# Query splits on GpSimd, value copies on ScalarE, and the first maxima reduced over two banks, in a graph layer followed by 128-head attention

## The chip, the cores and the metric

The kernel runs on one core of a Trainium2 chip. The metric is the device time of one execution in microseconds (us). Its engines have short names in the profile: PE is TensorE (matmuls), PEld its weight loads, DVE is VectorE, ACT is ScalarE, POOL is GpSimd, and SP is SyncE, which here only issues transfers (DMAs). Each engine works through its own queue in order, and waits on semaphores of the others. SBUF is the on-chip memory of 128 partitions; PSUM is the matmuls' output memory, in banks of 512 float32 for each partition.

## The reference

There are 3327 nodes with 128 features and a sparse weighted adjacency matrix `adj` (about 5 entries in a row). Layer 0 is a graph layer, layer 1 an attention of 128 heads of 8 numbers each:

```python
def reference(x, adj, W_in, W_out, Wq, Wk, Wv, Wo):
    x = _layernorm(x + _L0_gnn_ref(x, adj, W_in, W_out))
    x = _layernorm(x + _L1_gnn_ref(x, adj, adj, Wq, Wk, Wv, Wo))

def _L0_gnn_ref(X, A, W_in, W_out):
    return _message(X, A, W_in) + _message(X, A.T, W_out)   # A rows divided by their sum, then @ X @ W

def _L1_gnn_ref(x, spatial_encoding, edge_encoding, Wq, Wk, Wv, Wo):
    n, d = x.shape                         # 3327, 128
    h = Wq.shape[0] // d                   # 8
    q = (x @ Wq.T).reshape(d, n, h)
    k = (x @ Wk.T).reshape(d, n, h)
    v = (x @ Wv.T).reshape(d, n, h)
    a = jnp.einsum('dnh,dmh->dnm', q, k) * d ** (-0.5)
    a = jax.nn.softmax(a + spatial_encoding + edge_encoding, axis=2)
    out = jnp.einsum('dnm,dmh->dnh', a, v).reshape(n, h * d)
    return out @ Wo.T
```

The reshape to `(d, n, h)` cuts the flat product, so the rows of one tile of nodes belong to several heads: two tiles of 128 rows hold nearly ten heads.

## The kernel before

**Stages.** First layer 0 (lines 173 to 332): the matrix streams in twice, and PE sums it against x. Then the projections (lines 642 to 735) compute queries, keys and values of all nodes and store them in device memory. Then comes attention (lines 740 to 1325): a short opening in which the maxima of the first group of four heads are found alone, and a long loop of scores, exponentials and products (lines 1255 to 1325), in which the maxima of later groups are found beside. At the end the results are joined, projected and normalized.

**Projections.** Nodes are taken in 13 pairs of tiles (`t`), each with two halves (`s`), so 26 tiles of 128 rows. For a tile PE makes three products of 128x1024 into PSUM (line 689: `wq`, `wk`, `wv`). ACT copies queries and keys out (`full`, line 697). Both are then split into three bfloat16 parts whose sum is the float32 value (lines 712 to 717): the first part is a rounded copy on ACT (line 714), `left` is what remains (line 715, DVE), the second part is its rounded copy (line 716, ACT), the third what remains of that (line 717, DVE). The tile `left` has three buffers, `parts` three (one for queries, one for keys of a pair), `full` four. At the second half SP stores the parts (line 719, to `q_d` and `k_d`). A float32 copy goes out too: of queries by a copy on POOL (line 700), of keys by one on ACT (line 702), both stored by DMAs that POOL issues (line 703). Of the keys ACT takes squares (line 708), DVE sums them to sizes (line 710), and POOL issues their store (line 711). Values are copied out of PSUM by DVE (line 692) into one of two buffers `v_sb`, and SP stores them (line 693).

**Beside the projections** two threshold searches run (`early_of`, `select`, lines 440 to 574), one for 4 heads, one for 28. They look for the largest keys of each head: DVE compares all sizes with a middle value and counts (lines 472, 476), PE sums the counts over partitions (line 481), DVE moves the bounds (lines 493 to 503), ten times for each of two limits. Then keys get ranks (PE lines 535 and 536, DVE line 537), and the chosen keys of the first two groups are gathered by products with one-hot rows (`hots_of` line 608 on DVE, `fill_tile` line 617 on PE) after POOL has split them (`split_keys`, lines 595 to 598). In this stage a scheduler sets the order on each engine, by its own estimate of times; the program's order is only its start.

**First maxima.** For each group an item of work is one tile of queries and 512 chosen keys for two heads (`run_item`, lines 999 to 1035): two matmuls into two single banks of the pool `ps_m` (three banks), and two reductions by DVE, one for each bank. Until the first group's maxima are stored, items run one after another (line 1202) with nothing beside them but small steps (`fix`, `merge`). The pool `ps_e` (two buffers of two banks) is taken by scores (line 1271) once the long loop begins. From here on the order on each engine is written out by hand.

Of the kernel before, what the change touches and what calls it, by code (L numbers as in the profile page):

```python
# [9 lines left out]
F32 = mybir.dt.float32  # L10
# [4 lines left out]
ALU = mybir.AluOpType  # L15
AX = mybir.AxisListType
# [4 lines left out]
P = 128  # L21
# [4 lines left out]
H = 8  # L26
HEADS = D
G = NP * D
NB = 512
# [49 lines left out]
def gnn_layers(ctx: ExitStack, tc: tile.TileContext, x, adj, adjt, w_in, w_out, wq, wk, wv, wo, out):  # L79


    nc = tc.nc
# [85 lines left out]
    with ExitStack() as c0:  # L168
# [4 lines left out]
        with ExitStack() as c1:  # L173
# [102 lines left out]
            for t0 in range(0, NT, 2):  # L276
# [7 lines left out]
                    op=ALU.is_equal,  # L284
# [110 lines left out]
        groups, queries, for_maxima, stored = {}, {}, {}, set()  # L395
# [182 lines left out]
        def load_choice(pool, s):  # L578

            assert ranked.get(s) == NT  # L580
            first = max(f for f in rank_d if f <= s * GH)
            at = pool.tile([P, NT, GH], F32, name="at", bufs=2)
            nc.sync.dma_start(at, rank_d[first][:, s - first // GH])
            keys = pool.tile([P, GH, NT, H], F32, name="keys")
            for j in range(GH):
                head = (s * GH + j) * N
                nc.sync.dma_start(keys[:, j], kf_d[head : head + NP, :].rearrange("(p t) h -> p t h", t=NT))
            return at, keys
# [49 lines left out]
        def begin_fill(banks):  # L638
            for which in range(2):
                nc.tensor.matmul(banks[which], ident_b, nothing, start=True, stop=False)  # L640

        with ExitStack() as c1:
            stage = c1.enter_context(tc.tile_pool(name="stage", bufs=2, side="right"))
            vbuf = c1.enter_context(tc.tile_pool(name="vbuf", bufs=1, side="right"))
            ps_pr = c1.enter_context(tc.tile_pool(name="ps_pr", bufs=4, space=PSUM))
            v_sb = [vbuf.tile([P, D, VW], F32, name=f"v_sb{i}") for i in range(2)]
            for v in v_sb:
                nc.gpsimd.memset(v, 1.0)

            chooser = c1.enter_context(tc.tile_pool(name="chooser", bufs=1, side="right"))  # L650

            def early_of(first, n, g):
                yield from select(chooser, lambda: ps_pr.tile([P, H * D], F32, name="pr"), first, n, first)
                at, keys = load_choice(chooser, g)
                parts = split_keys(chooser, keys)
                yield
                packed = chooser.tile([P, KEPT], BF16, name="packed")
                for u in range(TCUTS):
                    pair = ps_pr.tile([P, H * D], F32, name="pr")
                    banks = [pair[:, :NB], pair[:, NB:]]  # L660
                    begin_fill(banks)
                    tiles = tiles_of_fill(u)
                    for t in tiles:
                        fill_tile(banks, parts, hots_of(chooser, at, t, 8), u, t, t == tiles[-1])
                        yield
                    end_fill(banks, packed, u)
                spread(g, packed)
                begin_all(("s", g))

            info = chooser.tile([P, NT, 2 * SLOTS], F32, name="info")  # L670
            for t in range(NT):
                nc.gpsimd.indirect_dma_start(
                    info[:, t], None, info_d, bass.IndirectOffsetOnAxis(ap=node[:, t : t + 1], axis=0)
                )
            nc.gpsimd.tensor_copy(near, info[:, :, :SLOTS])
            nc.gpsimd.tensor_copy(weight, info[:, :, SLOTS:])

            choosing = [(early_of(*EARLY[0], 0), 1, 8), (early_of(*EARLY[1], 1), 4, 9)]
            for t in range(NT // 2):
                g = slice(2 * t * P * D, 2 * (t + 1) * P * D)  # L680
                parts_of = {}
                for name in ("wq", "wk"):
                    parts_of[name] = stage.tile([P, PARTS, H, 2, D], BF16, name="parts", bufs=3)
                for s in range(2):
                    for name in ("wq", "wk", "wv"):
                        pr = ps_pr.tile([P, H * D], F32, name="pr")
                        rows = x1t[:, 2 * t * P : 2 * (t + 1) * P].rearrange("d (p s) -> d s p", s=2)[:, s]
                        for c, w in bank_cuts(H * D):
                            nc.tensor.matmul(pr[:, c : c + w], rows, ws[name][:, c : c + w], start=True, stop=True)
                        if name == "wv":  # L690
                            v = v_sb[s]
                            nc.vector.tensor_copy(v[:, :, :H], pr.rearrange("p (c h) -> p c h", h=H))
                            nc.sync.dma_start(v_d[g, :].rearrange("(p s c) w -> p s c w", p=P, s=2)[:, s], v)
                            continue

                        full = stage.tile([P, H, D], F32, name="full", bufs=4)
                        nc.scalar.mul(full.rearrange("p h c -> p (h c)"), pr, 0.5 * D**-0.5 if name == "wq" else 1.0)
                        flat = stage.tile([P, D, H], F32, name="flat", bufs=3)
                        if name == "wq":
                            nc.gpsimd.tensor_copy(flat, full.rearrange("p h c -> p c h"))  # L700
                        else:
                            nc.scalar.copy(flat, pr.rearrange("p (h c) -> p c h", h=H))
                        nc.gpsimd.dma_start(
                            (qf_d if name == "wq" else kf_d)[g, :].rearrange("(p s c) h -> p s c h", p=P, s=2)[:, s], flat
                        )
                        if name == "wk":
                            square = stage.tile([P, H, D], F32, name="square", bufs=1)
                            nc.scalar.activation(square.rearrange("p h c -> p (h c)"), pr, AF.Square)
                            size = stage.tile([P, D], F32, name="size")
                            nc.vector.tensor_reduce(size, square.rearrange("p h c -> p c h"), axis=AX.X, op=ALU.add)  # L710
                            nc.gpsimd.dma_start(size_d[g].rearrange("(p s c) -> p s c", p=P, s=2)[:, s], size)
                        sb = parts_of[name]
                        left = stage.tile([P, H, D], F32, name="left", bufs=3)
                        nc.scalar.copy(sb[:, 0, :, s], full)
                        nc.vector.tensor_sub(left, full, sb[:, 0, :, s])
                        nc.scalar.copy(sb[:, 1, :, s], left)
                        nc.vector.tensor_sub(sb[:, 2, :, s], left, sb[:, 1, :, s])
                        if s:
                            nc.sync.dma_start(
                                (q_d if name == "wq" else k_d)[:, g].rearrange("r (p c) -> p r c", p=P),  # L720
                                sb.rearrange("p a h s c -> p (a h) (s c)"),
                            )

                    for some, begins, times in choosing:
                        if t >= begins:
                            for _ in range(times):
                                next(some, None)
                group_of(0)
                for _ in range(4 if t else 0):
                    begin_next()  # L730
            for some, _, _ in choosing:
                for _ in some:
                    pass
            nc.scalar.activation(gain, weight, AF.Exp, scale=-2.0)
            nc.vector.tensor_scalar(gain, gain, -1.0, 1.0, op0=ALU.mult, op1=ALU.add)
# [4 lines left out]
    with c_att as c1:  # L740
# [5 lines left out]
        ps_e = c1.enter_context(tc.tile_pool(name="ps_e", bufs=2, space=PSUM))  # L746
        ps_m = c1.enter_context(tc.tile_pool(name="ps_m", bufs=3, space=PSUM))
# [223 lines left out]
        def run_item(kind, g, of, *where):  # L971
# [25 lines left out]
                yield  # L997
                return
            spend(dve=1.37)
            banks = [ps_m.tile([P, NB], F32, name="m") for _ in range(2)]  # L1000
            kept = k_kept[g % 2]
            rows = [slice(64 * (1 - y), 64 * (1 - y) + KR) for y in range(2)]
            if kind != "maxima":
                q, c = where
# [16 lines left out]
            mx, i, x, c = where  # L1021
            tile_of = slice(i, NP, NT) if of.shape[-1] == NP else slice(i * P, (i + 1) * P)
            c0 = 0 if c < TCUTS else TCUTS
# [6 lines left out]
                    stop=True,  # L1030
                )
            yield
            for y in range(2):
                nc.vector.tensor_reduce(mx[:, i, y, c - c0 : c - c0 + 1], banks[y], axis=AX.X, op=ALU.max)  # L1034
            yield

        chosen_all = []
# [156 lines left out]
        with tc.manual_schedule(engines={ENG.PE, ENG.Activation, ENG.DVE, ENG.Pool, ENG.SP}):  # L1194
# [60 lines left out]
            for g in range(NG):  # L1255
                for b, (n0, w) in enumerate(BLOCKS):
# [9 lines left out]
                    for t in range(NT):  # L1266
                        pt = P if t < NT - 1 else P - (NP - N)
                        e = [None] * GH
                        for x0 in range(0, 2, per):
# [12 lines left out]
                            m = iter(())  # L1282
# [5 lines left out]
                            if busy:  # L1288
                                taken += 1
                                m = next_item()  # L1290
# [310 lines left out]
```

## Time and profile before

| | us |
|---|---|
| three runs | 12242.42, 12248.63 (median), 12254.28 |
| the profiled execution's own time | 12249.46 |
| its span | 12247.8 |
| PE busy | 11301.5 (92%) |
| ACT busy | 10801.5 (88%) |
| DVE busy | 9320.2 (76%) |
| POOL busy | 3389.2 (28%) |

The profile is of one execution. Its span leaves out what lies before the first and after the last instruction. Busy shares are averages over stages that differ much: in 40 slices of 306 us each, of which a digit is the busy share in tenths, the first four hold layer 0, the projections and the opening of the attention:

```profile
PE   6646999999999999999999999999999999999986
DVE  9678787878787788788888887888788888777306
ACT  6431899999989999999999999999999999999993
POOL 0221111111111124444443344343434334211002
```

From the fifth slice on PE and ACT are over 90% busy; before it no engine is all the time. Line numbers stand as L692 for line 692; an arrow `out<-in` names tiles by the program's names.

### The profile page before, as it was taken

What the parts mean: (1) busy time and instruction counts of PE and PEld (TensorE: products, weight loads), DVE (VectorE), ACT (ScalarE), POOL (GpSimd) and SP (SyncE); (2) the same over time, 40 slices, a digit from 0 to 9 for tenths busy, and PEclk for the clock granted to TensorE, in tenths of its full rate; (3) what the DMA queues carried; (4) which work ended last, traced back from release to release, by engine and by line L of the source; (5) the groups of instructions that cost most, each with busy time, mean ns of one, the idle gap of its engine ahead of it and who ended that gap; (6) DMA issues with size and microseconds to landing.
All of it is one profiled execution on the core that took longest, in us unless ns stands there. A gap on an engine that the chain in (4) does not pass through costs nothing.

```text
span 12247.8 us, 237994 instructions
## 1 busy us (share of the span) xinstructions
PE 11301.5 (92%) x90246; PEld 3038.3 (25%) x90246; DVE 9320.2 (76%) x18121; ACT 10801.5 (88%) x11375; POOL 3389.2 (28%) x4073
## 2 busy tenths in 40 slices
PE   6646999999999999999999999999999999999986
PEld 3321222222222222222222222222222222222214
DVE  9678787878787788788888887888788888777306
ACT  6431899999989999999999999999999999999993
POOL 0221111111111124444443344343434334211002
PEclk8765999999999999999999999999999999999997
DMA  6562444444431122222222222222222222222104
GB/s 229 159 160 67 40 42 40 40 40 35 41 35 22 31 51 71 67 59 62 61 60 62 60 64 66 62 56 71 61 67 56 62 59 61 59 59 56 29 7 131
DMA packets 2221820, 783.21 MB, mean 64 GB/s; under 512 B 1844208, under 2 KB 2111475, under 8 KB 2213941
## 3 DMA queue, kind: packets, MB, share of 16 engines
q1 hardware_dynamic: 2137109, 434.44, 22.7%
q0 software_dynamic: 78816, 286.92, 7.4%
q10 hardware_dynamic: 4736, 46.52, 1.1%
q8 instruction: 712, 11.67, 0.4%
q14 instruction: 447, 3.66, 0.1%
HBM read 597.12 MB, written 187.86 MB: 64 GB/s over the span
## 4 chain that ended last, share of the span: by engine, by line
ACT 37%; PE 33%; issue 12%; DVE 9%; DMA 1%; SPq 0%; POOL 0%; ACTq 0%; DVEq 0%; POOLq 0%
ACT es L1295 35%; PE o L1225 17%; PE e_ps L1275 11%; DVE mx_top L1034 4%; PE m L1025 3%; DVE mx_rest L1034 1%; PE y L1353 1%; ACT es L1297 1%; DVE hot L608 1%; DVE o_sb L1234 0%; PE m L617 0%; PE m L1170 0%; DVE above L472 0%; SPq L418 0%; PE m L640 0%
## 5 line engine op out<-in xcount | busy, mean ns | idle before, releaser
L1295 ACT ACTIVATE es<-e_ps 128x1024 f32<-128x1024 f32 (+1 forms) x9984 | 9469.8, 1023 | 648.0 <-PE e_ps L1275 364.3
L1225 PE MATMUL o<-es,v 128*9 128x512 f32 x46592 | 5760.2, 567 | 33.2 <-DVE o_sb L1234 32.7
L1034 DVE TENSOR_REDUCE mx_top<-m 128x1 f32<-128x512 f32 x6656 | 4252.7, 684 | 1207.1 <-PE m L1025 1162.7
L1275 PE MATMUL e_ps<-q_e,k_st 50*128 50x512 bf16 (+1 forms) x23296 | 4270.8, 370 | 224.6 <-ACT es L1295 81.9
L1275 PEld LDWEIGHTS <-k_st 50*128 50x128 bf16 (+1 forms) x23296 | 1413.9, 95 | 6257.5 <-issue 5787.9
L1034 DVE TENSOR_REDUCE mx_rest<-m 128x1 f32<-128x512 f32 x2048 | 1308.8, 683 | 371.9 <-PE m L1025 367.7
L1025 PE MATMUL m<-k_kept,q_m 48*128 48x512 bf16 x6656 | 1428.0, 385 | 103.7 <-DVE mx_top L1034 53.1
L608 DVE TENSOR_SCALAR hot<-hot_no,at 128x336 bf16<-128x336 bf16 x3840 | 1297.4, 404 | 224.8 <-PE m L617 209.3
L844 POOL TENSOR_TENSOR slot_each<-hits,whole_q 128x832 f32<-128x832 f32 x256 | 425.6, 1662 | 2987.4 <-DVE hits L829 2972.3
L1225 PEld LDWEIGHTS o<-es,v 128*9 128x9 f32 x46592 | 696.2, 88 | 1557.6 <-issue 1443.6
L1297 ACT ACTIVATE es<-e_ps 128x1020 f32<-128x1020 f32 x832 | 809.2, 1024 | 72.9 <-PE e_ps L1275 54.1
L1025 PEld LDWEIGHTS <-q_m 48*128 48x128 bf16 x6656 | 508.7, 144 | 160.0 <-issue 153.7
L1234 DVE COPY o_sb<-o 128x512 f32<-128x512 f32 (+1 forms) x224 | 145.1, 648 | 527.9 <-PE o L1225 525.9
L1075 POOL DMA_INDIRECT near_rows<-kn_d,near x211 | 201.3, 954 | 1062.0 <-DVE prod L1085 985.4
L1025 PE MATMUL m<-k_kept,slot_rows_q 48*128 48x512 bf16 x2048 | 442.5, 385 | 33.1 <-DVE mx_rest L1034 26.4
L798 POOL TENSOR_TENSOR slot_each<-whole_q 128x416 f32<-128x416 f32 x64 | 57.8, 904 | 1462.7 <-DMA whole_q<-qf_d 1418.9
L1147 POOL TENSOR_TENSOR acc<-acc,prod 128x1024 f32<-128x1024 f32 x185 | 430.5, 2327 | 14.5
L242 PE MATMUL acc<-a_t,x 128*128 128x512 f32 (+1 forms) x728 | 311.3, 584 | 64.1 <-DMA a_t<-in_adj_dram 44.0
L1146 POOL TENSOR_TENSOR prod<-near_rows,s 128x1024 f32<-128x1024 f32 x185 | 365.9, 1978 | 2.5
L617 PE MATMUL m<-hot,parts 128*24 128x168 bf16 (+9 forms) x7200 | 289.3, 230 | 38.1 <-DVE hot L608 37.7
L1075 POOL DMA_INDIRECT near_rows<-vn_d,near x211 | 206.9, 981 | 346.5 <-DVE prod L1085 295.7
L1085 DVE TENSOR_TENSOR prod<-qn,near_rows 128x512 f32<-128x512 f32 x422 | 294.9, 699 | 0.0
(301 smaller groups left out, 6127.0 us busy)
## 6 DMA issues: line engine op xcount, KB each, us to landing
q_m<-q_d SPq DMA_DIRECT2D x768, 52.0 KB
q_e<-q_d SPq DMA_DIRECT2D x2304, 16.0 KB
a_t<-in_adj_dram ACTq DMA_DIRECT2D x13, 1663.5 KB
a_t<-in_adj_dram SPq DMA_DIRECT2D x13, 1663.5 KB
a_t<-in_adjt_dram SPq DMA_DIRECT2D x13, 1663.5 KB
a_t<-in_adjt_dram ACTq DMA_DIRECT2D x13, 1663.5 KB
q_d<-parts SPq DMA_DIRECT2D x13, 1536.0 KB
k_d<-parts SPq DMA_DIRECT2D x13, 1536.0 KB
```

Source lines behind the costliest of these rows:

```text
L242: nc.tensor.matmul(acc[:, b, :w], x0[:, t, :], a_t[:, n0 : n0 + w], start=t == 0, stop=t == NT - 1)
L608: nc.vector.tensor_scalar(hot, hot_no, at[:, t, j : j + 1], None, op0=ALU.is_equal)
L844: nc.gpsimd.tensor_mul(each, hits[y][:, i : i + 4, :, None].to_broadcast(shape), whole_q[:, y, None].to_broadcast(shape),)
L1025: nc.tensor.matmul(banks[y], of[rows[y], tile_of], kept[rows[y], x, c * NB : (c + 1) * NB], start=True, stop=True,)
L1034: nc.vector.tensor_reduce(mx[:, i, y, c - c0 : c - c0 + 1], banks[y], axis=AX.X, op=ALU.max)
L1075: nc.gpsimd.indirect_dma_start(rows.rearrange("p d h -> p (d h)"), None, table, bass.IndirectOffsetOnAxis(ap=rows_at, axis=0))
L1146: nc.gpsimd.tensor_mul(prod, vg, share)
L1147: nc.gpsimd.tensor_add(acc[:, :, :H], acc[:, :, :H], prod)
L1225: nc.tensor.matmul(o[32 * j : 32 * j + VW, :w], v4[:pt, j, t, :], e[j][:pt], start=t == 0, stop=t == NT - 1,)
L1275: nc.tensor.matmul(bank[:pt, y, x * NB // per : x * NB // per + w], k[r, x0 + x, t * P : t * P + pt], q[r, x0 + x, :w], start=True, stop=True,
L1295: nc.scalar.activation(es[:pt, :, :w], bank[:pt, :, :w], AF.Exp, scale=2.0)
L1297: nc.scalar.activation(es[:pt].rearrange(shape, x=per)[:, :, :, :w], bank[:pt].rearrange(shape, x=per)[:, :, :, :w], AF.Exp, scale=2.0,)
```

## The change

There are three edits. Value copies out of PSUM go from DVE to ACT. The last three steps of the split of queries, two subtractions and a rounded copy, go to POOL (before: DVE, ACT, DVE); keys are split as before. And until the first group's maxima are stored, an item's two matmuls write two banks of one buffer of `ps_e`, and one reduction takes both banks to two numbers.

```diff
                         if name == "wv":
                             v = v_sb[s]
-                            nc.vector.tensor_copy(v[:, :, :H], pr.rearrange("p (c h) -> p c h", h=H))
+                            nc.scalar.copy(v[:, :, :H], pr.rearrange("p (c h) -> p c h", h=H))
                             nc.sync.dma_start(v_d[g, :].rearrange("(p s c) w -> p s c w", p=P, s=2)[:, s], v)
...
                         nc.scalar.copy(sb[:, 0, :, s], full)
-                        nc.vector.tensor_sub(left, full, sb[:, 0, :, s])
-                        nc.scalar.copy(sb[:, 1, :, s], left)
-                        nc.vector.tensor_sub(sb[:, 2, :, s], left, sb[:, 1, :, s])
+                        if name == "wq":
+                            nc.gpsimd.tensor_sub(left, full, sb[:, 0, :, s])
+                            nc.gpsimd.tensor_copy(sb[:, 1, :, s], left)
+                            nc.gpsimd.tensor_sub(sb[:, 2, :, s], left, sb[:, 1, :, s])
+                        else:
+                            nc.vector.tensor_sub(left, full, sb[:, 0, :, s])
+                            nc.scalar.copy(sb[:, 1, :, s], left)
+                            nc.vector.tensor_sub(sb[:, 2, :, s], left, sb[:, 1, :, s])
...
             spend(dve=1.37)
-            banks = [ps_m.tile([P, NB], F32, name="m") for _ in range(2)]
+            pair = None
+            if (0, 0) not in stored and kind == "maxima":
+                pair = ps_e.tile([P, 2, NB], F32, name="e_ps")
+                banks = [pair[:, y] for y in range(2)]
+            else:
+                banks = [ps_m.tile([P, NB], F32, name="m") for _ in range(2)]
...
-            for y in range(2):
-                nc.vector.tensor_reduce(mx[:, i, y, c - c0 : c - c0 + 1], banks[y], axis=AX.X, op=ALU.max)
+            if pair is not None:
+                nc.vector.tensor_reduce(mx[:, i, :, c - c0], pair, axis=AX.X, op=ALU.max)
+            else:
+                for y in range(2):
+                    nc.vector.tensor_reduce(mx[:, i, y, c - c0 : c - c0 + 1], banks[y], axis=AX.X, op=ALU.max)
```

In the built program the order that the scheduler makes changes too. SP's queue has both stores of a pair's parts behind POOL's or DVE's last split. POOL's split of the gathered keys of the first group (lines 595 to 598) stands behind the splits of tile 8; before, it stood ahead of the copy of tile 7. SP's loads of the sizes for the search of 28 heads stand behind the values of tile 8; before, part of them stood behind the values of tile 6. On DVE the first instruction of a tile is now the sum of squares (line 710); before, it was the first subtraction of the queries.

## The prediction

> **What bounds the kernel now.** I read the busy time by stage first (columns: stretch in us; busy us of PE, its weight loads, DVE, ACT, POOL with instruction counts; clock; DMA share; GB/s).
>
> ```profile
> 0.00:438.80 438.80, 336.11 (x858) 164.34 (x858) 383.91 (x772) 251.90 (x180) 19.51 (x107) 0.89 0.58 211
> 438.80:1012.60 573.80, 262.21 (x1099) 119.45 (x1101) 385.13 (x879) 205.53 (x210) 138.48 (x145) 0.67 0.64 163
> 1012.60:1205.40 192.80, 171.81 (x322) 40.54 (x323) 184.99 (x333) 0.00 (x0) 45.66 (x82) 0.50 0.04 9
> ...
> 1228.60:12100.00 10871.40, 10445.79 (x87562) 2638.82 (x87561) 8247.64 (x15899) 10313.64 (x10921) 3148.56 (x3689) 0.99 0.29 53
> ```
>
> The change touches the second row (projections, 573.8 us) and the third (first group's maxima, 192.8 us). The long row below them runs the same instructions in the same order afterwards, so it only shifts. In the second row no engine is full: DVE is busy 385 of 574 us, POOL 138. In the third DVE is busy 96%. The chain that ended last joins the two:
>
> ```profile
> 989.69 1.14 DVE v_sb L692
> 990.83 2.31 SPq L719
> ...
> 993.24 12.64 DMA v_d<-v_sb
> ...
> 1008.27 4.14 DMA q_m<-q_d
> ...
> 1013.22 61.80 DVE mx_top L1034 x104
> ```
>
> Maxima wait until the last tile of the projections is stored, so every us won or lost before 1012.6 reaches the end. Which wait rules inside the stage is told by its waits (waiter, releaser: total us, times, longest):
>
> ```profile
> POOL flat L700 <- ACT full L697: 213.7, 19, 36.5
> ACT full L697 <- PE pr L689: 174.6, 27, 21.4
> PE pr L481 <- DVE count_of L476: 134.6, 27, 49.6
> ...
> POOL parts L595 <- DMA keys<-kf_d: 39.0, 1, 39.0
> ```
>
> This is one loop: ACT starts a tile when PE has its queries; PE, in order, is held by the sums of the threshold search (L481); these wait for DVE's counts (L476), which stand in DVE's queue between the splits. So a tile's period is DVE's queue plus a PE round trip: the 26 tiles start 14.4 to 18.0 us apart from 509 to 590, 22.5 to 28.5 apart from 657 to 835, and about 15 apart after that. The 39.0 us is POOL standing at L595 for keys while the next tile's copy waits behind it.
>
> **Prices.** DVE instructions of 1024 elements follow one another every 1.135 us (461.16, 462.30, 463.43 in DVE's time line). A tile loses three on DVE (two query splits, one value copy): 3 x 1.135 = 3.4 us, 26 tiles: 88.5 us. ACT loses a cast (1.046) and gains a value copy, which the trace shows only on DVE; the nearest ACT row, L702 out of PSUM, took 1.007, the cast 1.046: between -0.04 and 0.00 us a tile, taken as nothing. POOL gains two subtractions and a cast. The same three operations on 832 elements are there:
>
> ```profile
> L598 POOL TENSOR_TENSOR parts<-slot_each,parts 128x832 bf16<-128x832 f32 x32 | 57.6, 1798 | 2.6
> L596 POOL TENSOR_TENSOR slot_each<-keys,parts 128x832 f32<-128x832 f32 x32 | 56.6, 1768 | 2.6
> ...
> L597 POOL CAST parts<-slot_each 128x832 bf16<-128x832 f32 x32 | 28.2, 881 | 2.0
> ```
>
> Scaled by 1024/832 from their usual 1.76 and 0.88: 2.16 + 1.09 + 2.16 = 5.4 us a tile, 140 us in all; from below, L1146 of 1024 elements took 1.98, so 5.05. With the copy L700 (2.0) and three DMA issues (0.53 to 0.55) POOL has 9.0 us a tile, under every mean period above; POOL's busy time is no bound except where tiles come 7 us apart (958 to 966).
>
> **What POOL does to DVE** decides the sign. Two time lines, POOL's and DVE's (start, duration):
>
> ```profile
> 824.83 1.75 POOL L596 TENSOR_TENSOR slot_each<-keys,parts 128x832 f32<-128x832 f32 x1
> ```
> ```profile
> 825.04 1.59 DVE L502 COPY_PREDICATED limits<-few,middle 128x28 f32<-128x28 uint32 x1
> 826.55 0.18 DVE L503 COPY_PREDICATED low<-few,middle 128x28 f32<-128x28 uint32 x1
> ...
> 528.90 2.03 DVE L715 TENSOR_TENSOR left<-full,parts 128x1024 f32<-128x1024 f32 x1 [4.32 <-ACT parts L714]
> ```
>
> L502 takes 0.18 alone; here it ends when POOL's subtraction does. L715 takes 1.21 alone and 2.03 behind L700 (527.86 to 529.86). L537 shows it (three in 2.52, alone 0.18 each) and L608 (eight in 3.55 beside L700 at 904.3, eight in 1.82 without). So splits, threshold steps and one-hots on DVE stand still while POOL reads SBUF; the reduction L710 and copies out of PSUM don't.
>
> [...]
>
> **The sum, by stretches.** T is a tile's first ACT instruction.
>
> *Start, tiles 0 to 2.* POOL comes free at 476.5 (its gathers). The search of the first four heads needs the sizes of tiles 0 and 1, issued on POOL behind the moved splits of both: tile 0 takes 1.9 + 2.16 + 0.6 (issue) + 1.0 (L675, L676) + 1.09 + 0.55 + 2.16 + 0.6 = 10.1, tile 1 up to its size 1.9 + 2.16 + 0.55 + 1.09 + 0.55 + 2.16 = 8.4, so the second size leaves at 476.5 + 18.5 = 495.0 instead of 489.0 (+6). SP issues the loads of these sizes behind the query store, which now waits for POOL's last subtraction; a store of 1.5 MB is in front of them: +4. Together +10 (0 if hidden, 15 if DVE's two early key splits block POOL too).
>
> *Tiles 3 to 7.* Old: T+2.1 query subtraction, value copy, second query subtraction, L710 at T+6.5, the first key subtraction, first count ends at T+10.7, PE 4.3 us: next T at 15.0 (two counts) or 16.5 to 18.0 (three). New: DVE's first instruction is L710, which needs ACT's square: five ACT instructions, T+4.9 to 6.75. POOL meanwhile: L700 to 3.1, issue, subtraction 3.95 to 6.1, issue, cast 6.6 to 7.7. The key subtraction, ready at 6.75, stands until 7.7 and ends 8.85; POOL's second subtraction takes 8.85 to 11.0 and the threshold step (1.23) ends at 12.2. Next T: 12.2 + 4.3 = 16.5; with three counts, key split to 13.35, a step of 1.43, 14.8 + 4.3 = 19.1. Against 18.0, 15.0, 17.3, 16.5, 14.4: 1.1 + 1.5 + 1.8 + 2.6 + 2.1 = +9. With no lock felt, 13.7 and 16.4: -5. I take +9: L715's row shows the lock in nearly every tile.
>
> *Between tiles 8 and 9* (590 to 657, 67 us). In the new order POOL's L595 stands behind tile 8's splits, not before tile 7's copy, so tile 7's sizes are no longer late; but SP loads the sizes of 28 heads only after tile 8's values are stored, at T+7, and these loads pace each other at 9.5 us (572 to 602): about 37 + 2 us to landing, then two search steps and PE, 14: 60 us. -7 (-10 to 0).
>
> *Tiles 9 to 15.* The same walk puts the second key split at T+13.25, old T+12.0; some one-hots move into idle time. Seven tiles, 0 to +1 each: +3 (down to -1.3 x 7 = -9 without lock).
>
> *Tiles 16 to 20.* PE's projections are interleaved with ranks, each waiting for a short DVE addition (L537) that stands behind POOL: 5.4 us more of POOL in each, 2 felt: +10 (0 to 27).
>
> *Tiles 21 to 25 and the last stores.* Old DVE work from 887 on: 73 us plus about 11 standing. New: 53 plus POOL's 6 x 7.4, part of it under L710; fills end some 10 us later, and the key splits of the last pair still wait for the query store behind SP's twelve loads: +10 (-17 to +25).
>
> *Maxima.* 284 reductions came every 0.594 us (61.80/104); 142 instructions of 1024 at 1.135 each save 142 x 0.053 = 7.5, and with the 0.061 by which 0.594 exceeds 512 elements at 0.533, 8.6: -9. Cover: PE must refill a pair within 1.135; two matmuls into different rows took 0.62 + 0.21. If two pairs starve DVE by 0.1 us, +14 instead.
> [...]
>
> Sum: 10 + 9 - 7 + 3 + 10 + 10 - 9 = +26 on the profiled run's 12249.5 (span 12247.8), which lies 0.8 above the median of the runs, 12248.6: 12275.
>
> **Rivals.** *DVE relief wins*: POOL's extra work falls where DVE is idle (189 us of the stage) or reducing. For: DVE had to stand only where both came together. Against: the walk, where POOL's last subtraction lands on the threshold steps. Start +6, -5, -10, -9, later ten tiles half of 34, -17, maxima -9: -44, 12205. It decides if a tile's L476 ends before T+10.7. *A wash*: transfers pace the stage (keys, sizes, stores of 1.5 MB: ACT waited 30.2 us for query stores); for: 590 to 657; against: the loop above. Start +10, maxima -9: 12250. *Worse*: POOL bounds the last ten tiles (9.0 us plus some 2 standing, against 7 to 9 between starts from 871 to 887 and after 958), +20 to +30 more, or pairs starve, +23: about 12300.
>
> **How the numbers follow.** The forecast has 0.42 (own range 12255 to 12300), the worse case 0.18, the wash 0.15, relief 0.25. 0.2%, 24.5 us, is about what can be told from no change. Of the forecast 0.30 lies beyond it: slower 0.30 + 0.18 = 0.48; same 0.12 + 0.15 = 0.27; faster 0.25. Range 12205 to 12315: half of relief and a third of the worse case are outside.
>
> **What would show it.** Right: maxima start at 1040 to 1055 and take about 184 us; L502, L537, L608 and the key subtraction show durations near 2 us beside POOL; tiles 3 to 7 start 16.5 to 19 apart. Wrong: DVE's standing no longer than now, tiles closer than 15 us, or the stretch 590 to 657 shorter than 50 us.

## The result, and the profile after

| | before | after |
|---|---|---|
| median, us (range of 6 runs each) | 12247.0 (12242.42 to 12254.28) | 12295.17 (12286.69 to 12300.66) |
| ratio to before, 95% interval | | 1.0038 (1.0025 to 1.0051) |
| profiled execution, its span | 12249.46, 12247.8 | 12300.66, 12299.0 |
| the run of maxima reductions begins at | 1013.22 | 1062.81 |
| first store of maxima at | 1205.10 | 1246.86 |

The changed kernel is slower by 0.38%, 48 us by the medians. (Before, one reduction ran alone at 1010.56, ahead of the run.) By the last two rows the projections became 49.6 us longer and the maxima 7.8 shorter. What lies behind the first store of maxima took 11042.7 us before and 11052.1 after; in eleven other kernels of this study, which all run the same long loop there, it took 11033 to 11061 (in a twelfth 11119, on a chip where the kernel before took 0.6% longer too), so these 9 us are not put down to the change.

Busy time by stage, the projections of the kernel before first, then two stages of the changed kernel (columns as in the prediction: stretch; busy us of PE, weight loads, DVE, ACT, POOL with instruction counts; clock; DMA share; GB/s):

```profile
437.00:1013.22 576.22, 264.21 (x1106) 120.31 (x1106) 386.29 (x888) 206.89 (x213) 138.48 (x145) 0.67 0.64 163
```
```profile
437.00:1062.81 625.81, 266.26 (x1101) 119.37 (x1104) 409.64 (x807) 204.42 (x213) 278.45 (x223) 0.65 0.59 150
1062.81:1247.15 184.34, 96.35 (x321) 22.40 (x319) 176.29 (x190) 0.00 (x0) 45.66 (x82) 0.50 0.03 9
```

The first row of each is the projections. Before, DVE was busy 386.3 us. Now it has 78 instructions of 1024 elements less, 88.5 us of work at 1.135 each, and is busy 409.6. So DVE's other instructions took 409.6 + 88.5 - 386.3 = 112 us longer. POOL's load grew by 140.0 us. Below, "stood" is always worked out like this: DVE's busy time, plus 1.135 for each instruction removed, less the busy time of the kernel compared with. Where query subtractions were removed it is a little too low: 12 of the 52 first subtractions (L715) had themselves stood before, 1.47 to 2.05 us where 1.21 is usual. The chain that ended last still joins the stages as it did before, and the reductions now take pairs of banks, 1.133 us each (58.90/52):

```profile
1022.23 11.87 DMA q_d<-parts
...
1040.11 16.10 DMA k_d<-parts
1062.81 58.90 DVE mx_top L1044 x52
...
1129.35 53.17 DVE mx_top L1044 x47
```

DVE's groups in the projections show who stood (line, operation, shapes, count; busy us, mean ns; idle before), the kernel before first:

```profile
L715 DVE TENSOR_TENSOR left<-full,parts 128x1024 f32<-128x1024 f32 x52 | 72.1, 1389 | 63.5 <-ACT parts L714 63.5
L608 DVE TENSOR_SCALAR hot<-hot_no,at 128x336 bf16<-128x336 bf16 x240 | 62.6, 318 | 11.5 <-DMA at<-rank_d 6.7 <-PE pr L617 4.8
...
L502 DVE COPY_PREDICATED limits<-few,middle 128x4 f32<-128x4 uint32 x20 | 3.2, 162 | 0.0
```
```profile
L608 DVE TENSOR_SCALAR hot<-hot_no,at 128x336 bf16<-128x336 bf16 x240 | 98.8, 468 | 19.9 <-PE pr L617 15.6 <-DMA at<-rank_d 4.2
L710 DVE TENSOR_REDUCE size<-square 128x128 f32<-128x1024 f32 x26 | 48.9, 1882 | 2.5 <-ACT square L708 2.2 <-issue 0.3
L722 DVE TENSOR_TENSOR parts<-left,parts 128x1024 bf16<-128x1024 f32 x26 | 45.2, 1742 | 22.9 <-ACT parts L721 22.9
L720 DVE TENSOR_TENSOR left<-full,parts 128x1024 f32<-128x1024 f32 x26 | 44.4, 1712 | 12.0 <-ACT parts L714 12.0
...
L502 DVE COPY_PREDICATED limits<-few,middle 128x4 f32<-128x4 uint32 x20 | 16.6, 828 | 0.0
...
L500 DVE TENSOR_SCALAR few<-count_of 128x4 uint32<-128x4 f32 x10 | 10.5, 1052 | 0.3
...
L500 DVE TENSOR_SCALAR few<-pr 128x4 uint32<-128x4 f32 x10 | 1.6, 157 | 15.1 <-PE pr L481 15.1
```

The one-hots (L608) alone stood 36 us longer. L502 took 162 ns before. The two L500 rows are one operation of one size, once from SBUF (1052 ns, before 165) and once from PSUM (157 ns, before 156). The reduction L710 did not change (1882 ns, before 1885). One tile of the changed kernel shows it instruction by instruction, POOL first, then DVE (start, duration):

```profile
557.82 2.00 POOL L700 COPY flat<-full 128x1024 f32<-128x1024 f32 x1 [0.20 <-ACT full L697]
560.11 0.56 POOL L703 DMA_DIRECT2D qf_d<-flat  x1 [0.30 <-POOL flat L700]
560.69 2.14 POOL L716 TENSOR_TENSOR left<-full,parts 128x1024 f32<-128x1024 f32 x1
562.76 0.55 POOL L703 DMA_DIRECT2D kf_d<-flat  x1
563.31 1.51 POOL L717 CAST parts<-left 128x1024 bf16<-128x1024 f32 x1
```
```profile
557.95 1.90 DVE L494 TENSOR_SCALAR middle<-middle 128x4 f32<-128x4 f32 x1
559.88 0.27 DVE L472 TENSOR_TENSOR above<-room,middle 128x104 bf16<-128x104 f32 x1
560.18 0.26 DVE L476 TENSOR_REDUCE count_of<-above 128x4 f32<-128x104 bf16 x1
560.36 3.56 DVE L722 TENSOR_TENSOR parts<-left,parts 128x1024 bf16<-128x1024 f32 x1
563.85 0.15 DVE L500 TENSOR_SCALAR few<-pr 128x4 uint32<-128x4 f32 x1
```

L494, four elements and 0.17 us alone, ends with POOL's copy. The second key subtraction L722 ends 1.1 us after POOL's L716, and POOL's cast L717, 1.05 us alone, ends 0.9 us after L722: the two engines stand for each other.

### The profile page after: what moved, and what is told of

It reads as the page before. It is cut to its first block, busy times and chain, and to the rows that moved or that the text cites. A ratio compares the mean times of both kernels' runs of the same rounds, so it can differ in the third digit from the quotient of the medians.

```text
span 12299.0 us, 237870 instructions
## 1 busy us (share of the span) xinstructions
PE 11227.1 (91%) x90211; PEld 3021.0 (25%) x90246; DVE 9337.6 (76%) x17897; ACT 10800.0 (88%) x11375; POOL 3527.7 (29%) x4151
## 4 chain that ended last, share of the span: by engine, by line
ACT 37%; PE 34%; DVE 13%; issue 13%; DMA 1%; SPq 1%; POOL 0%; ACTq 0%; DVEq 0%; POOLq 0%
ACT es L1308 36%; PE o L1238 16%; PE e_ps L1288 10%; PE m L1035 3%; DVE mx_top L1047 3%; DVE hot L608 1%; DVE mx_top L1044 1%; DVE mx_rest L1047 1%; DVE top_at L252 1%; DVE top_w L251 1%; PE y L1366 1%; PE pr L689 1%; PE acc L242 1%; ACT es L1310 1%; DVE o_sb L1247 0%
## 5 line engine op out<-in xcount | busy, mean ns | idle before, releaser
L1047 DVE TENSOR_REDUCE mx_top<-m 128x1 f32<-128x512 f32 x6428 | 4115.2, 684 | 1190.6 <-PE m L1035 1166.6
L1047 DVE TENSOR_REDUCE mx_rest<-m 128x1 f32<-128x512 f32 x1984 | 1270.0, 684 | 370.0 <-PE m L1035 365.5
L608 DVE TENSOR_SCALAR hot<-hot_no,at 128x336 bf16<-128x336 bf16 x3840 | 1334.4, 414 | 233.6 <-PE m L617 209.7
L1035 PE MATMUL m<-k_kept,q_m 48*128 48x512 bf16 x6428 | 1300.3, 379 | 49.9 <-DVE mx_top L1047 45.6
L1035 PE MATMUL m<-k_kept,slot_rows_q 48*128 48x512 bf16 x1984 | 404.8, 378 | 28.3 <-DVE mx_rest L1047 23.9
L242 PE MATMUL acc<-a_t,x 128*128 128x512 f32 (+1 forms) x728 | 305.8, 576 | 67.2 <-DMA a_t<-in_adj_dram 47.2
L1159 POOL TENSOR_TENSOR prod<-near_rows,s 128x1024 f32<-128x1024 f32 x185 | 365.9, 1978 | 2.4
```

The lines of the kernel that those rows point to most:

```text
L242: nc.tensor.matmul(acc[:, b, :w], x0[:, t, :], a_t[:, n0 : n0 + w], start=t == 0, stop=t == NT - 1)
L608: nc.vector.tensor_scalar(hot, hot_no, at[:, t, j : j + 1], None, op0=ALU.is_equal)
L1035: nc.tensor.matmul(banks[y], of[rows[y], tile_of], kept[rows[y], x, c * NB : (c + 1) * NB], start=True, stop=True,)
L1159: nc.gpsimd.tensor_mul(prod, vg, share)
```

## The experiments

Two theories at first. *Standing*: the cost is DVE's time beside POOL. *Order*: the cost is the new order in the queues, or waiting for POOL's results. Ratios are to the kernel before on the same chip.

**The three parts alone, and two together.** Each edit is the part of the diff shown above, by itself.

> The kernel before with the value copies on ACT and nothing else. Standing theory (DVE stands still while POOL works in SBUF; the loss is the query split's alone): DVE gets 26 x 1.135 = 29.5 us less and POOL no more, so the stage is shorter or the same; with 26 copies of about 1.0 us more on ACT, which was 206 of 574 us busy, 0 to -25 us: 12222 to 12247, taken 12235. Order theory (the loss comes from the order in which instructions and transfers stand in the queues, which any of these edits changes): the stores of values now follow ACT's copy, and part of the +48 appears here: 12255 to 12275.

> The kernel before with the query split on POOL and nothing else. Standing theory: after, less the two helpful edits. The maxima took 7.8 us less in the trace of after, the value copies are worth 0 to 25 us, so this is slower than after: 12295 + 8 + 0 to 25 = 12303 to 12328, taken 12315. Order theory: about after less what the value copies contribute to the disorder, 12280 to 12303.

> The kernel before with the two-bank reduction alone. Both theories: the maxima stretch 192.2 to 184.3 us, nothing else moved: 12247 - 8 = 12239. If the gain is given back in the long loop (whose last exponentials came 7 us later in after, relative to the first ones), 12246.

> The change without the query split: value copies on ACT and the two-bank reduction. Standing theory: 12235 - 8 = 12227, faster than both kernels. Order theory: 12247 to 12267.

| kernel | median us | ratio, 95% |
|---|---|---|
| value copies on ACT alone | 12215.24 | 0.9972 (0.9961 to 0.9983) |
| query split on POOL alone | 12278.93 | 1.0026 (1.0015 to 1.0036) |
| two-bank reduction alone | 12241.52 | 0.9994 (0.9985 to 1.0003) |
| value copies and two banks | 12205.32 | 0.9965 (0.9951 to 0.9978) |
| before, in these runs | 12251.09 | |

The order theory missed the first and the last, and was the nearer one for the split alone. With two banks alone the maxima took 184.4 us, as in after; 10 us of median are within what these runs can tell. The value copies gain more than expected, and the split alone costs less than expected, 28 us over before, where the standing theory's 12303 to 12328 stands for 56 to 81 over its 12247. The three alone add up to -0.28 + 0.26 - 0.06 = -0.08%, 10 us faster; together they are 0.38% slower. So some 56 us are neither part's own. Without the query split the change is 46 us faster than before, and 90 faster than after.

**POOL's work without its use.**

```diff
 # value copies and two banks; then, for queries:
+ spare = stage.tile([P, H, D], BF16, name="spare", bufs=1)
+ nc.gpsimd.tensor_sub(spare, full, sb[:, 0, :, s])
+ nc.gpsimd.tensor_copy(spare, full)
+ nc.gpsimd.tensor_sub(spare, full, sb[:, 0, :, s])
```

> Value copies on ACT and the two-bank reduction (12205), queries split on DVE and ACT as before, and POOL does the three operations of a query split once more beside them, on the same inputs (twice a subtraction, once a rounded copy) into a spare tile that nobody reads. So POOL has after's load, DVE has no relief, and no store or split waits for POOL's results. Standing theory: DVE stands about as long as in after against the kernel without the split (DVE busy 409.6 + 59.0 removed - 364.9 = 104 us), and the stage follows: 12205 + 60 to 140, taken 12305. Waiting theory (what costs is that stores and the next steps wait for POOL's results): only the issues of sizes on POOL come later, 12205 to 12220.

Measured: 12309.28, ratio 1.0053 (1.0039 to 1.0066), with before at 12245.08. Nothing waits for what POOL computes here, and the loss is there, 104 us on the 12205. Its projections:

```profile
437.00:1072.75 635.75, 272.33 (x1105) 122.70 (x1105) 470.40 (x860) 229.96 (x239) 287.82 (x223) 0.65 0.58 148
```

DVE is busy 470.4 us, against 364.9 without POOL's extra work: 105.5 us of standing for 146.8 us of POOL. Its idle time did not grow (165.4 us, 179.1 without), so DVE did not wait longer, not for POOL's later DMA issues either. The waiting theory, 12205 to 12220, falls.

**Less of the split on POOL.** Once the middle copy goes back to ACT (`nc.scalar.copy(sb[:, 1, :, s], left)`), once only the last subtraction stays on POOL.

> After, with the middle rounded copy of the query split back on ACT, so that POOL has only the two subtractions. POOL's extra load falls by 26 x 1.05 = 27 us of 140. Standing theory: DVE stands 27 x 104/140 = 20 us less: 12275. Waiting theory: POOL's second subtraction now waits for a copy that stands in ACT's queue behind copies of the keys: 12295 to 12320.

> After, with only the last of the three steps of the query split on POOL; the first subtraction is DVE's and the rounded copy ACT's, as before. POOL's extra load is 26 x 2.25 = 58 us, DVE is relieved of 26 x 1.135 = 29.5. Standing theory: 58 x 104/140 = 43 us of standing less 29.5: +14 on the 12205 without the split, and up to +30 where the standing falls on threshold steps: 12219 to 12235. Waiting theory: the stores still wait for POOL, most of the +90 stays: 12260 to 12290.

Measured: 12241.38, ratio 0.9998 (0.9989 to 1.0007), and 12224.66, ratio 0.9983 (0.9974 to 0.9992). The second is as expected. The first gained 54 us, where 20 were expected. All kernels side by side, from 437 us to the run of maxima reductions (us; "stood" against the kernel with value copies and two banks, for the split alone against before):

| kernel | POOL busy | DVE busy | DVE relieved | stood | DVE idle | stretch |
|---|---|---|---|---|---|---|
| before | 138.5 | 386.3 | | | 189.9 | 576.2 |
| value copies, two banks | 141.0 | 364.9 | | | 179.1 | 544.0 |
| last subtraction on POOL | 196.6 | 368.0 | 29.5 | 32.6 | 194.2 | 562.2 |
| both subtractions on POOL | 252.8 | 365.9 | 59.0 | 60.0 | 207.7 | 573.6 |
| after | 278.5 | 409.6 | 59.0 | 103.7 | 216.2 | 625.8 |
| POOL's work unused | 287.8 | 470.4 | 0 | 105.5 | 165.4 | 635.8 |
| query split alone | 280.9 | 398.2 | 59.0 | 70.9 | 212.4 | 610.5 |

With one or both subtractions on POOL, standing takes back just what DVE is relieved of (32.6 for 29.5, 60.0 for 59.0). With the cast in between as well, 26 us more of POOL's work cost 44 us of standing. That POOL's second subtraction then no longer waits for ACT's cast (19.0 us in 23 waits with both subtractions on POOL) may be the reason; no run tests it. DVE's idle time grows as well, from 179 to 216 us, which the kernel with POOL's work unused doesn't show. In after search steps and one-hots wait longer for PE (waiter, releaser: us, times, longest):

```profile
DVE count_of L498 <- PE pr L481: 20.3, 14, 6.2
DVE few L500 <- PE pr L481: 20.0, 13, 6.3
...
DVE hot L608 <- PE pr L617: 15.6, 6, 5.4
```

In the kernel with value copies and two banks these are 5.6, 5.5 and 1.5 us: 43 us more here. The wait for the loads of the sizes (L485) is longer too, 47.2 us after 6.1, and the wait of the first subtractions for ACT's casts (L714) is shorter, 12.0 after 82.5; in all 37 us more. The waits for PE are as long with both subtractions on POOL (19.8, 19.8 and 17.3), so they are not what the cast adds.

**Two orders changed.** First the second search begins half a pair of tiles earlier, so that SP loads its sizes ahead of tile 8's stores; then SP instead of POOL issues the stores of the sizes.

```diff
- (early_of(*EARLY[1], 1), 4, 9)
+ (early_of(*EARLY[1], 1), 3.5, 9)
- if t >= begins:
+ if t + s / 2 >= begins:
```
```diff
- nc.gpsimd.dma_start(size_d[g]...
+ nc.sync.dma_start(size_d[g]...
```

> After, with the second threshold search (28 heads) begun in the program half a pair of tiles earlier, so that SP may issue its loads of sizes ahead of tile 8's stores. Between tiles 8 and 9 after took 72.4 us, the query split alone 50.1, and in after the loads left SP at 625.5, in the other from 584.7. If that place in SP's queue is what lengthened the stretch: 12295 - 20 = 12275. If the stretch follows DVE's standing: 12290 to 12300.

> After, with the stores of the sizes issued by SP in place of POOL. In after POOL waits 52.9 us at these issues for DVE's sums, with the last query subtraction behind them in its queue; in the kernel with the middle copy on ACT, which is 54 us faster, 25.8. If POOL's waiting for DVE, while DVE stands for POOL, is the part of the +90 that standing less relief (104 - 59 = 45 us) leaves open: 12295 - 20 to 40 = 12255 to 12275. If standing and its place alone set it: 12285 to 12300.

Measured: 12310.78, ratio 1.0053 (1.0039 to 1.0066), and 12301.32, ratio 1.0046 (1.0032 to 1.0059). Neither helps. The first moved the whole search up by a tile: the loads left SP at 608.6 instead of 625.1, but that is again 19.7 us after the start of the last tile ahead of them (tile 7, at 588.9; in after it is tile 8, at 605.1). The long gap now lies between tiles 7 and 8 (588.9 to 667.3, 78.4 us; after: 72.4 between 8 and 9), and the maxima began at 1075. So this run does not test loads that leave earlier against the tiles. In the second SP stands at the stores of the sizes in POOL's place (246.6 us for DVE's sums), and POOL's own wait there is not what costs. Why PE answers the search later in after is not settled.

**Does an instruction with a source in PSUM stand?** The first key subtraction reads PSUM (the program is otherwise that of after):

```diff
- nc.vector.tensor_sub(left, full, sb[:, 0, :, s])
+ nc.vector.tensor_sub(left, pr.rearrange("p (h c) -> p h c", h=H), sb[:, 0, :, s])
```

> After, with the first key subtraction reading the keys from PSUM and only their rounded copy from SBUF. In after these 26 subtractions took 1.71 us in the mean, at least 1.21. Standing theory, if what stands are instructions with two sources in SBUF or with copies from SBUF to SBUF, and not those that read PSUM (few from sums in PSUM took 0.16 in the mean beside POOL, few from counts in SBUF 1.05): each takes about 1.2, DVE stands up to 13 us less, part of it taken up by the next instruction: 12280 to 12295. If any instruction of DVE stands beside POOL, the mean stays at 1.7 and the time at 12295.

Measured: 12288.72, ratio 1.0037 (1.0023 to 1.0051). Its groups:

```profile
L722 DVE TENSOR_TENSOR parts<-left,parts 128x1024 bf16<-128x1024 f32 x26 | 50.0, 1926 | 8.3 <-ACT parts L721 8.3
...
L720 DVE TENSOR_TENSOR left<-pr,parts 128x1024 f32<-128x1024 f32 x26 | 31.5, 1213 | 17.4 <-ACT parts L714 17.4
...
L500 DVE TENSOR_SCALAR few<-count_of 128x4 uint32<-128x4 f32 x10 | 15.0, 1502 | 0.3
```

None of the 26 subtractions stands any more (1204 to 1225 ns, mean 1213, after 1712). But others do: L722 rose from 1742 to 1926 ns, L500 from 1052 to 1502. The subtractions were busy 12.9 us less, DVE in all only 5.8 (403.9 after 409.6), and the projections are as long as in after (625.6 us).

**No tile's work left on POOL.** Value copies and two banks, with the queries' float32 copy on ACT as well: `nc.scalar.copy(flat, full.rearrange("p h c -> p c h"))`.

> Value copies on ACT, the two-bank reduction, queries split on DVE and ACT, and the queries' float32 copy on ACT too, so that POOL has no copy or split of a tile left. Standing theory: the first query subtraction, which takes 2.03 us beside POOL's copy and 1.21 alone, gets its 1.21; all subtractions together stood 10 us in the kernel without this step (12205): 12192 to 12205. If ACT, which gets 26 x 1.0 us more, becomes the bound: 12215 to 12230.

Measured: 12218.83, ratio 0.9979 (0.9970 to 0.9988). Standing did go: DVE was busy 337.3 instead of 364.9 us. But the projections grew from 544.0 to 557.3 us, with ACT at 275 instead of 230 us busy. The time is that of the expectation's second case, but ACT is busy only half of the stage. The copy on POOL hides more than it costs; what it hides is not settled.

**The value copies back on DVE, the rest as after** (line 692 as before).

> After, with the value copies back on DVE. Alone these copies on ACT were worth 36 us (12215 against 12251). Filler theory: beside POOL's query splits a copy from PSUM is work that DVE can do while POOL has the port, so taking it away only makes DVE stand longer (DVE's standing against its own base was 71 us with these copies on DVE and 104 us without them): the query split alone gave 12279, less 8 to 9 us for the two-bank reduction: 12270, faster than after by 20 to 30 us. If the two edits add up, after without the copies on ACT is slower than after: 12295 + 36 = 12331.

Measured: ratio 1.0022 (1.0013 to 1.0031); the medians are 12351.33 and, for the kernel before on the chip of this run, 12323.71, so only the ratio is compared. On a before of 12247 it stands for 12274, 21 us faster than after, with intervals that just overlap; the sum of parts, 12331 or 1.0069, is far outside. DVE stood 76 us here (403.0 + 59.0 - 385.7, the last of the two-bank reduction alone), against 104 in after. The copies out of PSUM themselves don't stand:

```profile
L692 DVE COPY v_sb<-pr 128x1024 f32<-128x1024 f32 x26 | 31.7, 1219 | 67.0 <-PE pr L689 65.1 <-PE pr L536 1.7 <-issue 0.3
```

Before they took 1217 ns; here 18 of the 26 ran at least in part while POOL computed, and the longest took 1.23 us. So copies out of PSUM are work that DVE can do beside POOL's split; what POOL holds meanwhile, the expectation's "port", no run shows. Taken away, they are replaced by standing: 29.5 us of copies are gone, and 27 us of standing come. From tile 9 to the maxima after takes 385.3 us, this kernel 386.1 and the split alone 384.8: 17 copies less on DVE gain nothing.

That after is slower than this kernel comes from another place, between tiles 8 and 9: 72.4 us in after, 48.4 here, 50.1 in the split alone. This outweighs the 7 us that after gains from tile 3 to 8. There SP's queue differs. Three of the four loads of sizes leave SP from 583.8 us on here and from 584.7 in the split alone; in after all four leave from 625.1 on. No run changes this order alone, so it is not shown that it is the cause.

## Why the prediction was right in sign and short in size

Slower was the likeliest side, and 12295 lies within the range and near the top, 12300, of the forecast's own. The sum was +26 where the trace has +42 up to the first store of maxima:

| stretch | predicted | measured |
|---|---|---|
| up to tile 3 | +10 | +16.8 |
| tiles 3 to 8 | +9 | -1.6 |
| tiles 8 to 9 | -7 | +5.0 |
| tiles 9 to 16 | +3 | +19.0 |
| tiles 16 to 21 | +10 | +13.5 |
| tile 21 to the maxima | +10 | -3.1 |
| maxima | -9 | -7.8 |

- *Prices.* POOL's subtractions took 2.14 and 2.29 us and its cast 1.11, where 2.16 and 1.09 were scaled from 832 elements. ACT's value copy took 1.02.
- *What POOL does to DVE.* That DVE stands beside POOL was right, shown by the unused work on POOL, and what stands was rightly told apart. The "lock" of the prediction's walks is in no trace; the runs show lengthened instructions. It took L715's row to show it in nearly every tile, but only 12 of the 52 subtractions there took 1.47 to 2.05 us instead of 1.21. Of 140 us of POOL, 112 were felt, more than DVE's relief of 88.5, and DVE's idle time grew by 26 besides (216.2 after 189.9). The traces have both sides: the same subtraction took 1213 ns with one source in PSUM and 1712 with both in SBUF, and POOL's cast took 1.51 us beside DVE's L722, 1.05 alone.
- *Tiles 9 to 15* is the step that failed, by 16 us: "some one-hots move into idle time". They stood instead. In this stretch 120 one-hots went from 32.1 to 46.4 us, and DVE waited 13.3 us more for PE to read them.
- *Between tiles 8 and 9.* The order was as predicted, the start of the loads was not: T+7 was taken, and T+20 came, as SP's queue in after shows (T = 605.1):

```profile
614.53 0.38 SPq L724 DMA_DIRECT2D k_d<-parts  x1
614.96 7.46 SPq L418 DMA_DIRECT2D v<-v_d  x1
622.51 2.52 SPq L693 DMA_DIRECT2D v_d<-v_sb  x1
625.13 30.25 SPq L454 DMA_DIRECT2D room<-size_d  x4
```

The key store in front of them waited for the last key subtraction, which stood (2.28 us), and a load of values then held the queue for 7.5 us. The 13 us are about the 12 by which this term is off; that they are its cause is not shown, since no run has the loads earlier with the rest as in after.
- *Start.* +17 was outside the 0 to 15 given. The second size left POOL at 491.5, earlier than the 495.0 of the sum, and the loads left SP 5 us later than before (496.6 after 491.3); but DVE's first sum of what they brought ran at 516.6 instead of 499.8. SP spent 18.4 us on the two loads of sizes, 6.9 before (to 515.0 and 498.2); the sum had +4 for the store in front of them and nothing for this.
- *Tiles 3 to 8 and the end* were over-priced, by 11 and 13 us: the walk for one tile was too slow for the first (18.8, 12.4, 20.3, 14.8 and 13.3 us between starts, where it had 16.5 or 19.1), and the ten last tiles came in time in spite of POOL's 9 us each.
- *The relief, 88.5 us*, was summed as if each of the three instructions were worth the same. The 26 value copies were worth 36 us alone, and beside the split after is about 21 slower for their going to ACT: the text had said that copies out of PSUM don't stand, but not that these are what DVE does meanwhile.
- *Maxima.* -7.8 for -9: 142 reductions at 1.133 with no starved pair. The 0.533 for 512 elements is in the traces as the difference of two mean durations, 1210 ns of a pair (L1044) and 677 of a single bank (L1034).
- *Signs.* The maxima took 184 us as said, and L502, L537 and L608 show up to 2.30, 2.63 and 2.75 us beside POOL. But the maxima began at 1063, not at 1040 to 1055, and three of the five starts from tile 3 to 8 were less than 15 us apart, which the prediction had named a sign of being wrong: its picture of these tiles was.
- *Rivals.* Relief's 12205 was measured without the split; that is chance, since its sum was for the whole change. The wash falls with the 104 us of unused work. The worse case, POOL as the bound of the last ten tiles, asked for 40 us or more from tile 16 on, and 10 were measured; no pair starved. That 12295 is also near this case's 12300 is chance.

## What to carry to other kernels

Work moved from DVE to POOL was not simply gone from DVE here, where both read SBUF: by the table of kernels DVE stood 0.50 to 0.75 us for each us that POOL took on, and POOL took about twice as long for a subtraction (2.14 us for 1.135). Before a copy out of PSUM is taken from DVE, look whether it is what DVE does while its other work would stand (here such copies took at most 1.23 us, 18 of the 26 at least in part while POOL computed). A change of several parts can hold a good one: here two of three gave 12205, the fastest kernel of the study.

## What the runs showed of the hardware

POOL stood for DVE too: the copy of POOL's work in the unused split took 1.91 us beside a DVE subtraction (554.16 to 556.07) and 1.05 alone. An earlier recorded start did not settle who went first: L722 is recorded from 560.36, POOL's L716 from 560.69, and L722 was the one that stood (3.56 us; L716 took 2.14, as in the mean). Nor did every instruction of one kind stand alike: the second of two conditional copies (L503) took at most 0.19 us in all 40 cases of after, the first (L502) up to 2.30. That is no property of the second, which took up to 2.55 us with POOL's work unused.
